# Both ends of a fused attention kernel: other orders and loads at the front, batch 0's transposes a step later, moves ahead of loads and two copies on VectorE at the end

## The chip, the core and the metric

The kernel runs on one core of one Trainium2 chip. The metric is the device time of one execution in microseconds. It was taken in three runs of the kernel, and one more execution was profiled. PE is TensorE, DVE is VectorE, ACT is ScalarE, POOL is GpSimd; SP issues most DMAs.

## What is computed

A residual attention layer over 64 batch items of 128 tokens with 512 features. There are 16 query heads of width 64 and one shared key and value head, with one extra "null" key and value in front of the 128 keys. The two layer norms use eps 1e-5.

```
xn   = layernorm(x) * g_in
q    = (xn @ Wq) as 16 heads of 64, times 1/8;  k, v = halves of (xn @ Wkv)
k, v = [null_k, k], [null_v, v]                       # 129 keys
sim  = q k^T + [null_bias, attn_bias]                 # 16 x 128 x 129
sim  = causal mask, and the batch item's key mask (the null key is always seen)
out  = softmax(sim) v, heads joined, @ Wo
y    = x + layernorm(out) * g_out
```

`null_k` and `null_v` are rows 0 and 1 of the input `cond`; all of it is 32-bit floating point.

## The kernel before

The function writes out, for each engine, one long list of instructions by hand. Each engine takes its own list in order and an instruction waits on semaphores for its inputs and for its buffers. So the order in which `step(n)` calls its helpers is the order on every engine, and an instruction that waits holds up all that is behind it on its engine.

**Steps.** The batch items come in 16 groups of four. The loop runs `step(n)` for n from -6 to 62. `step(n)` works on several items at once: it loads and normalises items some ten ahead, makes a part of the queries of group `(n + 6) // 4`, the keys and values of item n + 6, the scores of item `nb` (n + 2, later n + 3), the softmax of item `eb` (n + 1, later n + 2), the weighted sum of the values of item n, and the output projection of item n - 1 or of a pair of items. Steps -6 to 0 are the fill (`fill` in the code); here there are no values yet to be summed, and the queries of group 0 are plain products (`q_plain`, 3.4 us each, two in each of steps -6 to -3). From group 1 on, seven smaller products (`product`, with sums of tokens from `token_sum` and sums of weights from `weight_sums` and `weight_sum_3`) stand for eight. The output projections of items 1 to 58 are made for two items at a time in the same manner (`out_product`); item 0 and the items from 59 are made alone (`out_mm`, `out_stats`, `residual`). The constant `B3` is 58, and steps 57 to 61 have lines of their own.

**Normalising the input.** `norm_stats(m)` makes mean and variance on DVE and the reciprocal root on POOL (`pow`). `norm_apply(m)` scales on DVE for the first four items, on ACT from then on, with a factor `nmr` from DVE. `norm_T(m)` transposes on PE, and ACT copies the result out of PSUM. Items 8 and later go through a DVE transpose (`tokens_T`) and DMAs instead.

**Weights.** Each of the four parts of `wq` is scaled by `weights_q(kc)` (L842 to 850). The null key is worked into the key/value weights: POOL multiplies a part of `wq` with it (`weights_kv_prod`, L863), DVE scales `wkv`, sums the product and writes it in another order (`weights_kv`, `null_order`). `causal(u)` writes the causal mask into one half of the bias after its load.

**Softmax.** `bias_add` (POOL) writes bias plus key mask into the buffer `S[b]`, and `null_copy` (POOL) adds the null column; the tag "s" has two buffers. `scores` (PE) makes half of the scores, `scores_add` and `scores_max` (DVE) follow, `exps` takes one ACT instruction a row for eight rows in a half, and then come `rinv` (DVE) and `scale` (POOL). The scores live in one PSUM buffer of their own, so a second half waits for the first half's `scores_add`.

**Transposing the weights of attention.** Items 0 and 1 use PE: `attn_T_pe` (L606) transposes into PSUM and DVE copies to `aTb`. All later items use a DVE transpose (`blocks_T`, 1.77 us) and 14 small DMAs (`blocks_move`, L579), on SP's queue; for item 63 every second one goes to ACT's queue (`take`). `values` and `values_end` (PE) make the weighted sums, and ACT copies them out with the null value added (L680). In a step that goes on with scores, `values` waits for a tiny DVE copy, `done` (L668).

**Loads.** The loads of tokens, weights and bias are issued at the start; `load_second` (L175) follows when the first four items are under way, and `load_late` loads `wo` and `gob` after step -6. `transfers()` issues the stores of single items, residual loads and token loads of a step.

Of the kernel before, what the change touches and what calls it, by code (L numbers as in the profile page):

```python
# [17 lines left out]
def kernel(  # L18
# [156 lines left out]
    def load_second():  # L175
        nc.sync.dma_start(out=nbh, in_=null_bias.partition_broadcast(P))
        nc.sync.dma_start(out=nvb, in_=cond[1].partition_broadcast(P))
        load_mask(0)
        for m in (4, 5, 6):
            load_x(m)  # L180
        load_bias(1)
        for r in range(2):
# [206 lines left out]
    def weight_sum_3():  # L389
        nc.gpsimd.tensor_tensor(s3, a11, a21, ALU.subtract)  # L390
# [282 lines left out]
    def values_end(b, split):  # L673
# [5 lines left out]
        for u in range(2):  # L679
            nc.scalar.activation(  # L680
                oT[b][:, u * NF : (u + 1) * NF, :].rearrange(
                    "p f (s q) -> p s f q", q=Q
                ),
                po[u].rearrange("p h i f q -> p (h i) f q"),
                AF.Identity,
                bias=nv2,
            )
# [123 lines left out]
    def out_stats(b):  # L811
# [11 lines left out]
        if b == B - 1:  # L823

            nc.vector.scalar_tensor_tensor(y, y, rstd, res.pop(b), ALU.mult, ALU.add)
        else:
            yr[b] = y, rstd
# [8 lines left out]

    def store(b):
# [4 lines left out]
    def weights_q(kc):  # L842
        if kc < 2:
# [18 lines left out]
    def weights_kv_prod(kc):  # L862
        prods[kc] = sp.tile([P, H, DH], FP, tag="s", name=f"prod_{kc}")  # L863
# [15 lines left out]
    def step(n):  # L879
# [5 lines left out]
        mns = [m for m in (n + 10, n + 12) if ok(m) and (m >= 2 * GB) == (m == n + 12)]  # L885
# [27 lines left out]
        elif ok(nb) and n >= 0 and n != 1:  # L913
            bias_add(nb)
            null_copy(nb)
        if third:
            pair_pow(p4)
        for m in mns:
            norm_stats(m)
        if fast and f == 0 and fill:  # L920
            for k in range(1, 5):
                token_sum(qg, k)
            if n == -2:
                weight_sum_3()
# [3 lines left out]
        if ok(nb) and n < 0:  # L928
            null_copy(nb)
        if n == B3:  # L930
# [4 lines left out]
        if one:  # L935

            out_mm(n - 1, 0, NF if n > B3 + 1 else NC)
            if n == 1:
                attn_T_pe(1)
                bias_add(nb)  # L940
                null_copy(nb)
                out_stats(0)
# [11 lines left out]
        if soft:  # L954
# [17 lines left out]
        if soft:  # L972
# [3 lines left out]
        if soft and n != B3 + 1:  # L976
# [26 lines left out]
        if soft:  # L1003
# [8 lines left out]
        if n == B3:  # L1012
# [273 lines left out]
```

## Time and profile before

| what | before |
|---|---|
| three runs, us | 1126.49, 1126.77, 1124.78 |
| median, us | 1126.49 |
| the profiled execution, us | 1125.21 |
| its span, us | 1123.4 |
| PE busy | 1086.8 us, 97% of the span |
| DVE busy | 806.8 us, 72% |
| POOL busy | 745.0 us, 66% |
| ACT busy | 678.2 us, 60% |
| granted TensorE clock | 0.996 |

The profile shows one execution. Its page gives the busy time of each engine, and the busy share of each in 40 slices of 28 us. A row of the timeline is: start and duration in us, engine, line, operation, out and in with shapes, count, and in brackets the idle time of the engine just before it and what ended that. A row of the stretches gives the busy time of every engine between two points of the span, then the granted clock, the DMA share and the rate. Lines are those of the kernel before. Each 32-bit matrix product shows as two instructions. Neighbouring instructions of one kind are drawn together in one row, so a duration with a count above one spans all of them.

### The profile page before, as it was taken

The page shows a single profiled execution, that of the slowest core. Times are in us where ns is not written, and L with a number is a line of the kernel's source. Part 1 is how long each engine was busy: PE and PEld are TensorE (multiplying, and loading weights), DVE is VectorE, ACT ScalarE, POOL GpSimd, SP SyncE. Part 2 cuts the span into 40 slices and gives each one's busy share as a digit, 9 for nine tenths or more (in the row PEclk, how much of TensorE's full clock was granted, in tenths as well). Part 3 has the DMA queues.
Part 4 walks back from the last instruction along what each step waited for, and adds up shares of the span by engine and source line. Part 5 has one row for each costly group of instructions (what it writes and reads, how often), then busy time and mean ns, then how long its engine had stood idle before and what let it go on. Part 6 is the DMA issues. An engine that isn't in the chain of part 4 may idle for free.

```text
span 1123.4 us, 27505 instructions
## 1 busy us (share of the span) xinstructions
PE 1086.8 (97%) x9780; PEld 872.6 (78%) x9780; DVE 806.8 (72%) x1741; ACT 678.2 (60%) x2710; POOL 745.0 (66%) x588
## 2 busy tenths in 40 slices
PE   6888999999999999999999999999999999999987
PEld 4465788888888888888888888788888888888643
DVE  6564677786787777778777777877777886666762
ACT  2345656666675666676565667566567756657661
POOL 5454877667675676767577676657768575777832
PEclk9999999999999999999999999999999999999999
DMA  6313244353444435345343634534353453422333
GB/s 186 123 33 97 66 132 122 88 163 97 136 127 126 118 91 169 101 125 135 123 123 92 167 104 125 130 120 117 101 163 103 127 134 108 104 77 77 96 104 103
DMA packets 107864, 130.09 MB, mean 116 GB/s; under 512 B 29264, under 2 KB 72528, under 8 KB 105936
## 3 DMA queue, kind: packets, MB, share of 16 engines
q1 hardware_dynamic: 106480, 126.96, 40.1%
q8 instruction: 78, 1.28, 0.5%
q10 hardware_dynamic: 1248, 1.38, 0.4%
q14 instruction: 58, 0.48, 0.1%
HBM read 54.86 MB, written 31.46 MB: 77 GB/s over the span
## 4 chain that ended last, share of the span: by engine, by line
PE 82%; DVE 4%; DMA 4%; ACT 3%; POOL 2%; SPq 2%; issue 1%; ACTq 0%; POOLq 0%; DVEq 0%
PE pa L422 17%; PE pyX L750 16%; PE pyY L750 8%; PE pc L422 8%; PE ps L495 8%; PE po L636 7%; PE pk L308 5%; PE pw L422 4%; PE pyw L750 4%; PE py L697 3%; ACT s L522 2%; DMA x<-in_x_dram 2%; SPq L601 2%; DMA nbh<-cond_null_attn_bias_dram 1%; POOL xS L404 1%
## 5 line engine op out<-in xcount | busy, mean ns | idle before, releaser
L522 ACT ACTIVATE s<-s,nmax 128x65 f32<-128x65 f32 (+1 forms) x1024 | 372.1, 368 | 0.4
L466 POOL TENSOR_TENSOR s<-biasp,mneg 128x1536 f32<-128x1536 f32 x64 | 221.1, 3456 | 109.5 <-DVE sb L575 98.1
L543 POOL TENSOR_TENSOR s<-s,rinv 128x512 f32<-128x512 f32 (+1 forms) x128 | 189.3, 1480 | 119.3 <-DVE nmro L794 91.4
L680 ACT ACTIVATE oT<-po,nv 128x512 f32<-128x512 f32 x128 | 81.1, 684 | 199.4 <-PE po L636 199.4
L522 ACT ACTIVATION_READ_ACCUMULATOR s<-s,nmax 128x1 f32 x1024 | 194.6, 190 | 0.0
L750 PE MATMUL pyX<-wT,oT 128*128 128x256 f32 x696 | 164.7, 379 | 0.5 <-DVE kyu L762 0.5
L750 PEld LDWEIGHTS pyX<-wT,oT 128*128 128x128 f32 x696 | 131.8, 190 | 19.6 <-DVE kyu L762 0.9
L495 PEld LDWEIGHTS ps<-kT,qT 64*64 64x64 f32 x4096 | 94.5, 135 | 46.4 <-DVE s L508 24.2
L508 DVE TENSOR_TENSOR s<-ps,s 128x512 f32<-128x512 f32 (+1 forms) x128 | 121.5, 949 | 9.0 <-PE ps L495 8.7
L422 PE MATMUL pa<-xS,wq 128*128 128x256 f32 x480 | 123.7, 380 | 2.0 <-POOL wq L390 1.0
L513 DVE TENSOR_REDUCE nmax<-s 128x8 f32<-128x520 f32 (+1 forms) x128 | 120.1, 939 | 5.1 <-POOL s L475 3.7
L495 PE MATMUL ps<-kT,qT 64*64 64x64 f32 (+1 forms) x4096 | 118.9, 252 | 3.8 <-DVE s L508 3.1
L636 PE MATMUL po<-aTb,vs 64*64 64x256 f32 (+1 forms) x1240 | 118.5, 382 | 2.3 <-DVE done L668 2.2
L575 DVE STREAM_TRANSPOSE sb<-s 128x1536 f32<-128x1536 f32 x62 | 110.0, 1774 | 12.9 <-POOL s L543 3.6
L433 ACT COPY ku<-pa 128x256 f32<-128x256 f32 x120 | 44.8, 373 | 93.2 <-PE pa L422 93.2
L422 PEld LDWEIGHTS pa<-xS,wq 128*128 128x128 f32 x480 | 86.7, 190 | 12.3 <-ACT ku L433 1.6
L308 PE MATMUL pk<-wkv,xT 128*128 128x144 f32 x488 | 69.9, 286 | 0.0
L443 DVE TENSOR_TENSOR qT<-pw,kp 128x256 f32<-128x256 f32 x60 | 25.4, 424 | 61.4 <-ACT kp L433 61.3
L422 PE MATMUL pa<-xS,wS 128*128 128x256 f32 x240 | 67.8, 405 | 0.0
L636 PEld LDWEIGHTS po<-aTb,vs 64*64 64x64 f32 (+1 forms) x1240 | 57.0, 135 | 12.8 <-issue 3.9
L246 POOL TENSOR_TENSOR rstd<-rstd,nhalf 128x1 f32<-128x1 f32 x64 | 35.8, 560 | 42.9 <-DVE rstd L245 42.8
L422 PE MATMUL pc<-xS,wS 128*128 128x256 f32 x240 | 61.9, 380 | 1.9 <-POOL xS L404 1.9
(120 smaller groups left out, 2101.1 us busy)
## 6 DMA issues: line engine op xcount, KB each, us to landing
aTb<-sb SPq DMA_DIRECT2D x369, 64.0 KB
x<-in_x_dram SPq DMA_DIRECT2D x64, 256.0 KB
res<-in_x_dram SPq DMA_DIRECT2D x64, 256.0 KB
out_dram<-y SPq DMA_DIRECT2D x64, 256.0 KB
aTb<-sb SPq DMA_DIRECT2D x492, 32.0 KB
xd<-xb SPq DMA_DIRECT2D x14, 1024.0 KB
xT<-xd SPq DMA_DIRECT2D x56, 256.0 KB
wo<-in_L_cond_Wo_dram SPq DMA_DIRECT2D x1, 2048.0 KB
```

What stands on the lines that cost most here:

```text
L308: nc.tensor.matmul(pkv, xT[g][:, t, kc, :], wkv[:, kc, :], start=(kc == 0), stop=(kc == KC - 1),)
L422: nc.tensor.matmul(prod[tag], w[:, kc, f * P : (f + 1) * P], t[:, :, kc, :], start=(start and kc == 0), stop=(kc == HK - 1), skip_group_ch ...
L466: nc.gpsimd.tensor_tensor(S[b][:, :, 1 : ROW - 1], biasp, mneg[g][:, t].unsqueeze(1).broadcast_to([P, R8, NL + N]), ALU.add,)
L495: nc.tensor.matmul(pv[u * DH : (u + 1) * DH, r, f, :], qT[g][rows, f, t, hf, u], kT[b][rows, 0:nk], start=True, stop=True,)
L508: nc.vector.tensor_tensor(sv, pss.pop((b, hf)), sv, ALU.add)
L513: nc.vector.tensor_reduce(nmax[b][:, hf], S[b][:, :, WITH_NULL[hf]], AX.X, ALU.max, negate=True)
L522: nc.scalar.activation(row, row, AF.Exp, bias=nmax[b][:, hf, k : k + 1], accum_out=rsum[b][:, hf, k : k + 1],)
L543: nc.gpsimd.tensor_tensor(sv, sv, rinvs.pop((b, hf)).unsqueeze(2).broadcast_to([P, R8, sv.shape[2]]), ALU.mult,)
L575: nc.vector.transpose(sb.rearrange("p j e q -> p e j q"), S[b][:, :, 1 : ROW - 1].rearrange("p e (j k) -> p e j k", k=Q),)
L636: nc.tensor.matmul(pos[b][u][r * DH : (r + 1) * DH, half], vals[keys, b % GB, 0:DH], aT_of(b)[keys, slots, r * NF : (r + 1) * NF], start=s ...
L680: nc.scalar.activation(oT[b][:, u * NF : (u + 1) * NF, :].rearrange("p f (s q) -> p s f q", q=Q), po[u].rearrange("p h i f q -> p (h i) f q"),
L750: nc.tensor.matmul(prod[key], h[:, c, :], w[:, c, :], start=(start and c == 0), stop=(c == HC - 1), skip_group_check=not start,)
```

## The change

The front gets another order of loads, weights and norms. VectorE scales three parts of `wq` and ACT one; VectorE makes `weight_sum_3`; item 6 is normalised a step earlier, and its transpose keeps its place; the null value's negation, the null biases, the clearing of `aTb` and the loads of `wo` come later. The transposes of item 0 move from the end of step -1 into step 0, and bias and exponentials of items 1 to 3 get other places. At the end, the copies of items 61 and 62 are VectorE's, the moves of item 60 are split over two queues, moves come ahead of `transfers()`, several operations of steps 58 to 61 change places, and the last item's output is made in two halves of 256 columns.

```diff
 def load_second():
-    nbh; nvb; load_mask(0); x 4, 5, 6; load_bias(1); nv2
+    x 4, 5, 6; load_bias(1); load_mask(0); nbh; nvb; nv2
 def weight_sum_3():
-        nc.gpsimd.tensor_tensor(s3, a11, a21, ALU.subtract)
+        nc.vector.tensor_tensor(s3, a11, a21, ALU.subtract)
 def values_end(b, split):
         for u in range(2):
+            if b in (B - 3, B - 2):
+                nc.vector.tensor_scalar(o, v, nv2, None, ALU.add)
+            else:
+                nc.scalar.activation(o, v, AF.Identity, bias=nv2)
 def weights_q(kc):
-        if kc < 2:
+        if kc != 1:
             nc.vector.tensor_scalar(
 def weights_kv_prod(kc):
-        prods[kc] = sp.tile([P, H, DH], FP, tag="s", name=f"prod_{kc}")
+        pool, tag = ((sp, "s"), (sp, "s"), (hp, "sb"), (hp, "xb"))[kc]
+        bufs = None if kc < 2 else 1
+        prods[kc] = pool.tile([P, H, DH], FP, tag=tag, name=f"prod_{kc}", bufs=bufs)
+def last_output():
+        b = B - 1
+        halves = []
+        st = small.tile([P, 2, 6], FP, tag="st2", name="st2", bufs=1)
+        for e, (pool, tag) in enumerate(((ps_y, "Y"), (ps_w, "w"))):
+            cols = (lo_e, hi_e)[e]
+            py = pool.tile([P, HE], FP, tag=tag, name=f"py_{b}_{e}")
+            for c in range(NC):
+                nc.tensor.matmul(py, oT[b][:, c, :], wo[:, c, cols],
+                    start=(c == 0), stop=(c == NC - 1))
+            nc.vector.bn_stats(st[:, e], py)
+            halves.append((py, cols))
+        ...
+        for py, cols in halves:
+            nc.vector.scalar_tensor_tensor(
+                y[:, cols], py, mv[:, 0:1], gob[:, cols], ALU.subtract, ALU.mult)
+        r = res.pop(b)
+        for py, cols in halves:
+            nc.vector.scalar_tensor_tensor(
+                y[:, cols], y[:, cols], rstd, r[:, cols], ALU.mult, ALU.add)
+            nc.sync.dma_start(out=out[b][:, cols], in_=y[:, cols])
 def step(n):
-        mns = [m for m in (n + 10, n + 12) if ok(m) and (m >= 2 * GB) == (m == n + 12)]
+        mns = [... and m != 6]
-        elif ok(nb) and n >= 0 and n != 1:
+        elif ok(nb) and n > 1:
             bias_add(nb)
             null_copy(nb)
+        if fast and f == 0 and fill:
+            if n == -2:
+                weight_sum_3()
+            for k in range(1, 3):
+                token_sum(qg, k)
         for m in mns:
             norm_stats(m)
-        if fast and f == 0 and fill:
-            for k in range(1, 5):
-                token_sum(qg, k)
-            if n == -2:
-                weight_sum_3()
         ...
         if ok(nb) and n < 0:
             null_copy(nb)
+        if fast and f == 0 and fill:
+            for k in range(3, 5):
+                token_sum(qg, k)
         ...
             if n == 1:
                 attn_T_pe(1)
-                bias_add(nb)
-                null_copy(nb)
-                out_stats(0)
         ...
         if last:
             product(last_g, last_f, 4, ps_q, "a", start=False)
-        if soft:
+        if n == 1:
+            exps(eb, 0)
+            rinv(eb, 0)
+            scale(eb, 0)
+            exps(eb, 1, 0, 4)
+            bias_add(nb)
+            null_copy(nb)
+            out_stats(0)
+        elif soft:
             exps(eb, 0, 0, 4)
         ...
             q_out(last_g, last_f, hi_t, "c", "u2")
+        if n == 0:
+            attn_T_pe(0)
+            bias_add(nb)
+            null_copy(nb)
         ...
         if n == B3:
             scores(eb, 0)
             scores_add(eb, 0)
             scores_max(eb, 0)
             out_product(p12, 2, ps_w, "w")
+            out_part(p12, 0, "w", "yp1")
             pair_norm(p4)
+            scores(eb, 1)
+            scores_add(eb, 1)
             pair_residual(p4)
             store(p4)
-            out_part(p12, 0, "w", "yp1")
-            scores(eb, 1)
-            scores_add(eb, 1)
             exps_half(eb, 0)
-            scores_max(eb, 1)
         ...
             exps(eb, 1, 6)
-            rinv(eb, 1)
-            scale(eb, 1)
-        if third and n != B3:
+            if n <= B3 + 1:
+                rinv(eb, 1)
+                scale(eb, 1)
+        if third and n < B3:
             pair_norm(p4 + 1)
         ...
         if n == B3 + 1:
             blocks_T(n + 1)
-            blocks_move(n + 1)
+            blocks_move(n + 1, take=0)
         if soft and second:
             exps(eb, 1, 4)
+            if n == B3 + 1:
+                blocks_move(n + 1, take=1)
         ...
         if ok(n + 1) and fill:
-            exps(n + 1, 1)
+            exps(n + 1, 1, 0, R8 if n == 0 else 2)
         if sc and n != B3:
             scores(nb, 0)
             scores_add(nb, 0)
-            if ok(n + 1) and fill:
-                rinv(n + 1, 1)
-                scale(n + 1, 1)
         if ok(n):
             values(n, split)
+        if n == 0:
+            rinv(1, 1)
+            scale(1, 1)
+        if n == B3 + 2:
+            pair_norm(p4 + 1)
+            rinv(eb, 1)
+            scale(eb, 1)
         ...
-        if soft:
+        if soft and n != B3 + 3:
             blocks_T(eb)
         ...
             keep("a", "u2")
+        if n == -1:
+            exps(0, 1, 2)
         if ok(n) and not split:
             values_end(n, split)
+            if n == B3 + 3:
+                rinv(eb, 1)
+                scale(eb, 1)
+                blocks_T(eb)
         if n == B3:
             out_sums(p12)
             scores(nb, 0)
             scores_add(nb, 0)
+            scores_max(eb, 1)
             pair_norm(p4 + 1)
             pair_residual(p4 + 1)
         ...
-        late = first and fast
+        late = fast and (first or n < 0)
         if sc:
             scores(nb, 1)
             scores_add(nb, 1)
+            if n == -1:
+                rinv(0, 1)
+                scale(0, 1)
         ...
+        if n > B3 and eb in sbs:
+            blocks_move(eb)
         if n >= B3:
             transfers()
         ...
-        if n == -1:
-            attn_T_pe(0)
 # the start
+    keep_busy(14)
     norm_stats(0)
-    norm_stats(1)
     norm_apply(0)
     norm_T(0)
+    norm_stats(1)
     norm_stats(2)
+    keep_busy(4)
     norm_apply(1)
     norm_T(1)
     norm_stats(3)
+    keep_busy(2)
     norm_apply(2)
     norm_T(2)
-    keep_busy(8)
+    keep_busy(2)
     norm_apply(3)
     norm_T(3)
-    keep_busy(10)
+    keep_busy(3)
     load_second()
     weights_q(2)
     weights_q(0)
     weights_q(3)
     weights_q(1)
-    nc.gpsimd.memset(aTb, 0.0)
-    for kc in range(2):
-        weights_kv_prod(kc)
-    nc.vector.tensor_scalar(vnb[:, 0:DH], nvb, -1.0, None, ALU.mult)
-    null_order(vnb[:, DH:], nbh)
-    causal(1)
-    load_bias(0)
+    weights_kv_prod(0)
     for n in range(-6, B - 1):
         step(n)
         if n == -6:
+            for kc in range(1, KC):
+                weights_kv_prod(kc)
+            causal(1)
+            load_bias(0)
             for kc in range(2):
                 weights_kv(kc)
-            for kc in range(2, KC):
-                weights_kv_prod(kc)
-            load_late()
         if n == -5:
             for kc in range(2, KC):
                 weights_kv(kc)
             causal(0)
             mask_neg(0)
+            nc.vector.tensor_scalar(vnb[:, 0:DH], nvb, -1.0, None, ALU.mult)
+            null_order(vnb[:, DH:], nbh)
+            norm_stats(6)
+            norm_apply(6)
             weight_sums()
+        if n == -4:
+            nc.gpsimd.memset(aTb, 0.0)
+            load_late()
 # the end
-    out_mm(B - 1)
-    out_stats(B - 1)
-    store(B - 1)
+    last_output()
```

More of the change, by code (lines that the diff above doesn't have):

```diff
@@ L175, in load_second @@
     def load_second():
-        nc.sync.dma_start(out=nbh, in_=null_bias.partition_broadcast(P))
-        nc.sync.dma_start(out=nvb, in_=cond[1].partition_broadcast(P))
-        load_mask(0)
         for m in (4, 5, 6):
@@ L181, in load_second @@
         load_bias(1)
+        load_mask(0)
+        nc.sync.dma_start(out=nbh, in_=null_bias.partition_broadcast(P))
+        nc.sync.dma_start(out=nvb, in_=cond[1].partition_broadcast(P))
         for r in range(2):
@@ L679, in values_end @@
         for u in range(2):
[L680 to L687, printed above, removed]
+            o = oT[b][:, u * NF : (u + 1) * NF, :].rearrange("p f (s q) -> p s f q", q=Q)
+            v = po[u].rearrange("p h i f q -> p (h i) f q")
+            if b in (B - 3, B - 2):
+                nc.vector.tensor_scalar(o, v, nv2, None, ALU.add)
+            else:
+                nc.scalar.activation(o, v, AF.Identity, bias=nv2)
     def out_mm(b, lo=0, hi=NC):
@@ L822, in out_stats @@
         )
[L823 to L827, printed above, removed]
+        yr[b] = y, rstd
         ys[b] = y
@@ L835, in residual @@
         nc.gpsimd.tensor_tensor(y, y, res.pop(b), ALU.add)
+    def last_output():
[6 more added lines that the diff above has]
+            for c in range(NC):
+                nc.tensor.matmul(
+                    py,
+                    oT[b][:, c, :],
+                    wo[:, c, cols],
+                    start=(c == 0),
+                    stop=(c == NC - 1),
+                )
+            nc.vector.bn_stats(st[:, e], py)
+            halves.append((py, cols))
+        mv = small.tile([P, 2], FP, tag="mvo", name=f"mvo_{b}")
+        nc.vector.bn_aggr(mv, st)
+        rstd = small.tile([P, 1], FP, tag="rstdo", name=f"rstdo_{b}")
+        nc.vector.tensor_scalar(rstd, mv[:, 1:2], EPS, None, ALU.add)
+        nc.gpsimd.tensor_tensor(rstd, rstd, nhalf, ALU.pow)
+        y = hp.tile([P, DIM], FP, tag="y", name=f"y_{b}", bufs=3)
+        for py, cols in halves:
+            nc.vector.scalar_tensor_tensor(
+                y[:, cols], py, mv[:, 0:1], gob[:, cols], ALU.subtract, ALU.mult
+            )
+        r = res.pop(b)
+        for py, cols in halves:
+            nc.vector.scalar_tensor_tensor(
+                y[:, cols], y[:, cols], rstd, r[:, cols], ALU.mult, ALU.add
+            )
+            nc.sync.dma_start(out=out[b][:, cols], in_=y[:, cols])
     def store(b):
@@ L884, in step @@
         mkv, mk, mb = n + 6, n + 5, n + 11
-        mns = [m for m in (n + 10, n + 12) if ok(m) and (m >= 2 * GB) == (m == n + 12)]
+        mns = [
+            m
+            for m in (n + 10, n + 12)
+            if ok(m) and (m >= 2 * GB) == (m == n + 12) and m != 6
+        ]
         q, f = ok(qg, NG), part
@@ L971, in step @@
                 tokens_out(mb // GB)
-        if soft:
+        if soft and n != 1:
             exps(eb, 0, 4)
@@ L975, in step @@
             token_sum(qg, 1)
-        if soft and n != B3 + 1:
+        if soft and n not in (1, B3 + 1):
             rinv(eb, 0)
@@ L1002, in step @@
             q_plain(qg, 2 * f)
-        if soft:
+        if soft and n != 1:
             exps(eb, 1, 0, 2)
@@ L1029, in step @@
             out_part(p12, 0, "w", "yp1")
-        if soft:
+        if soft and n != 1:
             exps(eb, 1, 2, 4)
@@ L1090, in step @@
             store(p4 + 1)
-        if soft:
+        if soft and n != B3 + 3:
             blocks_T(eb)
```

## The prediction

> **What bounds the kernel now.** I read the page's busy rows, then PE by stretches, then the timeline of the badly filled stretches, then the chain at the end.
>
> ```profile
> PE 1086.8 (97%) x9780; PEld 872.6 (78%) x9780; DVE 806.8 (72%) x1741; ACT 678.2 (60%) x2710; POOL 745.0 (66%) x588
> ...
> PE   6888999999999999999999999999999999999987
> ...
> 17.97:47.52 29.55, 26.02 (x88) 13.35 (x87) 19.62 (x43) 8.73 (x14) 16.66 (x13) 1.00 0.47 128
> 47.52:66.98 19.46, 16.51 (x125) 10.75 (x124) 7.70 (x24) 5.54 (x12) 10.69 (x10) 1.00 0.18 53
> 66.98:81.00 14.02, 11.93 (x141) 9.03 (x140) 10.55 (x24) 8.21 (x38) 3.67 (x4) 1.00 0.07 20
> 81.00:93.97 12.97, 10.80 (x130) 8.55 (x127) 7.93 (x17) 8.73 (x38) 8.88 (x6) 1.00 0.54 155
> 93.97:117.00 23.03, 21.40 (x182) 14.23 (x180) 12.43 (x26) 10.15 (x42) 11.74 (x9) 0.93 0.14 35
> ```
>
> PE is full from slice 5 to 38: the middle can't be shortened by order. Columns of the stretches: length, then busy PE, PEld, DVE, ACT, POOL. PE's idle time, length minus busy: 3.5 + 3.0 + 2.1 + 2.2 + 1.6 = 12.4 us between the first query product (17.97) and the end of step 1 (117.0). Before 17.97 PE has only four token transposes to do. These 12.4 us and part of the 17.97 are all that the front can give. The timeline says what holds it (start, duration; in brackets the wait before):
>
> ```profile
> 11.69 1.38 POOL L1215 MEMSET aTb<- 128x1536 f32 x1
> 11.77 1.57 DVE L253 TENSOR_SCALAR x<-x,mv,rstd 128x512 f32<-128x512 f32 x1 [0.44 <-POOL rstd L246]
> 13.27 1.40 DVE L844 TENSOR_SCALAR wq<-wq,gin 128x1024 f32<-128x1024 f32 x2
> 16.42 2.19 ACT L848 ACTIVATE wq<-wq,gin 128x1024 f32<-128x1024 f32 x2
> 17.97 7.03 PE L373 MATMUL pq<-xT,wq 128*128 128x512 f32 x16
> ...
> 25.23 2.42 DVE L872 TENSOR_SCALAR wkv<-wkv,gin 128x128 f32<-128x128 f32 x1
> ...
> 42.73 0.66 PE L268 MATMUL pxT<-ident,x 128*128 128x128 f32 x4 [2.24 <-ACT x L259]
> ...
> 63.44 2.35 POOL L390 TENSOR_TENSOR wq<-wq 128x1024 f32<-128x1024 f32 x1
> 65.98 0.69 DVE L513 TENSOR_REDUCE nmax<-s 128x8 f32<-128x520 f32 x1 [3.72 <-POOL s L475]
> ...
> 90.30 0.66 PE L636 MATMUL po<-aTb,vs 64*64 64x256 f32 x8 [2.17 <-DVE done L668]
> ...
> 104.75 0.37 ACT L440 COPY qT<-pa 128x256 f32<-128x256 f32 x1 [8.98 <-PE pa L422]
> ...
> 119.20 3.45 POOL L466 TENSOR_TENSOR s<-biasp,mneg 128x1536 f32<-128x1536 f32 x1 [3.16 <-DVE mneg L452]
> ```
>
> A plain VectorE scaling takes 0.54 (the first three tokens), but 1.57 beside the memset; a 128x128 one takes 0.28 alone and 2.42 beside a POOL product that starts at 25.21. So some VectorE forms wait until POOL's instruction ends. And an in-order engine is stopped by its first waiting instruction: DVE by batch 0's null column (3.72), PE by `done` queued behind a reciprocal (2.17), ACT for 8.98 behind a query copy while PE does 6.9 us of `out_mm(0)`. At the end:
>
> ```profile
> 1076.62 1.98 PE L495 MATMUL ps<-kT,qT 64*64 64x128 f32 x32 [2.31 <-DVE s L508]
> ```
>
> and in the chain of waits (start, us, what)
>
> ```profile
> 1079.45 7.21 PE py L697 x16
> ...
> 1107.34 10.51 PE py L697 x24
> ```
>
> From 1079.4 to 1117.9 PE is in the chain nearly alone; before it DVE stops PE once more.
>
> **The change part by part, front.** Times are my schedule for the new order from these durations, against the same point before.
>
> Start: without the memset, token 3's scaling is 0.54: done at 12.3. DVE then scales parts 2, 0, 3 of wq (0.74 each): 13.05, 13.8, 14.5; ACT only part 1 (1.14). The ACT queue's two parts have landed by 9 us, SP's by about 11. Transposes 0.60, copy 0.59: first query product at 13.7, 4.2 earlier. The 14 more keep-busy instructions (50 for 36, 0.11 each) fill PE's idle time: 0. Moving three loads behind x and bias costs nothing: mask, nbh and nvb are first read near 32 us, and the wait of DVE for nvb (1.27, then 3.4 of slowed small copies) goes.
>
> Steps -6 and -5: two query products (6.87) and a transpose of 0.6 each. Now products 1 to 3 of the null key run back to back on POOL, 17.1 to 24.2 (2.35 each), then causal(1) 1.7; four of DVE's eight small operations meet them and wait up to 2.4 each. DVE reaches token 5's statistics at about 26.5 (28.96 before; 24.4 if it gets two operations between POOL's). Its transpose comes at 29.2, 1 us after PE could do it; step -4 starts at 29.85 for 33.45: 3.6 earlier.
>
> Step -4: norm 6 now stands ahead of `weight_sums` (3.7 us DVE), so the 2.24 wait goes; next late is token 8's statistics and then kv_out, at about 40.0. PE's three key/value products end at 42.2 for 47.6: 5.4. After it the memset (1.38) and two bias adds (6.9) stand ahead of token 7's power on POOL: its transpose waits 0.8: 4.4. SP: wo and gob now follow x9 and stand ahead of x10, x11 and the nv moves; 2 MB at the 400 GB/s of the first loads is 5 us, wo is first read in step 0 over 25 us later, nv 13 us later: 0 (0.6 us of issue at most).
>
> Step -2: `weight_sum_3` leaves POOL (2.35) and is 1.22 on DVE by rows L385 to 387. Those ran while POOL was idle; now POOL's token sums run beside it. Here a rule speaks against the change: by the Trainium skill, "SBUF — State Buffer", section Who interferes with whom, a DVE instruction with two SBUF inputs contends with a GpSimd instruction that reads SBUF, and the second waits. By the row DVE pays 1.2, by the rule up to 2.5 (one token sum of 1.27 more); no row here shows this pair. I take 1.3, keep 2.5 for the range: the sum falls from 11 to about 10. The null column now stands ahead of token sums 3 and 4, so the 3.72 goes, and product 7 has no 1.0 wait. End of step -2 at 59.4 for 66.98: 7.5.
>
> Steps -1 and 0: the transposes of batch 0 (2.1 us PE) move from -1 to 0 behind two products, so they no longer wait for the scale (0.9), but bias_add(2) (3.45) moves behind them too. Splitting exps 2+6 lets product 6's copy pass 2.3 us of ACT. Still ACT: 16 exps (5.8), copies and a norm make -1 end at 69.1, and the next product waits 1.2 for its last copy. Step 0: rinv(1,1) behind `values` ends the 2.17 wait, but values_end's copies stand behind eight exps, 1 us of PE. End at 84.2 for 93.97: 9.8.
>
> Step 1: exps(2, first half) and four more pass the query copy of 8.98 wait and run during `out_mm(0)`. DVE's rinv waits behind batch 1's transposed copies, so POOL starts with its scale only at about 94.3, then bias_add(3), power, scale, residual, weight sum: 10.8 us. PE ends at 103.9 for 117.0: 13.1. But DVE (maximum, kT, mask) ends 2 us later in relation to PE, so bias_add(4) comes at 108.1 for 119.2: 11.1. From here POOL is 99% busy for 30 us and leads the chain to the product at 134.8, so 11.1 is what remains. Later steps to 57 keep their order: 0.
>
> **End.** Step 58: out_part ahead of pair_norm frees the bank for which PE waited 0.9, but scores_max(60,1), 1.23, comes before pair_residual(56), for which PE waits next at about 1055.5 as before: 0 (-1 to +1). Step 59: half of batch 60's moves on the ACT queue: seven issues took 4.86 there for batch 63 (row of 1095.72); ACT was idle 3.50 before oT(59). So oT(59) and exps(62) come 1.3 late, of which I put 0.6 on PE; ends 0 and 4.9. SP is freed of 4.6 and the moves pass loads that blocked it 3.4: relief. Step 60: rinv and pair_norm(58) behind the score add: 0.2 for the two and 0.92 of waiting for exps go, -1.1. Two oT copies on DVE (about 0.7 each, idle there) let PE start without 0.32, and moves ahead remove an issue wait of 0.27. The last output: two halves of 8 products, the same 6.9 us; statistics of one half 0.42 for 0.70, then 0.2, 0.2 and four passes of 0.45 instead of two of 0.75: 2.6 us for 2.6; a last store of half the size, -0.1. Sum: -1.1 - 0.3 - 0.3 - 0.1 + 0.6 = -1.2.
>
> Together -12.3. The profiled execution took 1125.21 (span 1123.4 and 1.8 around it); 1112.9. It lies 1.3 under the median 1126.49, which would give 1114.2. I say 1113.5, 12.3 under 1125.8, the middle of the two.
>
> **Rivals.** (a) POOL holds the gain back: the wait for scale(2,0) at the head of POOL's queue in step 1 plus the lock of DVE; POOL starts step 2's chain only 4 us earlier. For it: 99% POOL to 150 us; against: POOL was idle 5.88 in step 1. 1125.8 - 4 - 1.2 = 1121. (b) DVE gets two operations between POOL's and ACT's waits shrink: nearly all of PE's 12.4 goes, with the 4.2 of the start 15, and 2 at the end: 1125.8 - 17 = 1109. (c) Slower: POOL in steps 0 and 1. bias_add(2) now waits for batch 0's transposes and bias_add(3) for scale(2,0), which waits for DVE behind batch 1's. Each us by which bias_add(4) slips is one at the end; it decides once bias_add(4) starts after 119.2 + 1.2 instead of 108, so 12.3 us of slip, from a chain whose own work is 10.8. At 5 us past that point: 1131. The rows speak against it, since DVE and ACT inputs are ready before. (d) The orders don't bite, everything waits as before for something not seen: 1126.
>
> **Numbers.** Forecast 0.50, (a) 0.20, (b) 0.20, (c) 0.06, (d) 0.04. Faster 0.90, same 0.04, slower 0.06; 0.2%, 2.3 us, is about what a measurement of this kernel can tell from no change. The forecast's own bounds (two-input wait 1.3, T5 and T7 1.8, ACT issues 4.3) give 1109 to 1119; with most of (a) and (b) 1107 to 1121.5.
>
> **What would show it.** Right: first query product near 13.7; token 3's scaling 0.54; no 3.72 and 2.17 wait; exps(2) inside `out_mm(0)`; bias_add(4) near 108; PE's end 1.2 closer to it than 998.7 us. Wrong: wkv or null copies of 2.4 each past 27 us; bias_add(4) later than 114; POOL the cause of PE waits after 110; oT(59) waiting on ACT's issues by more than 2 us.

## The result and the profile after

The changed kernel takes 1121.75 us (median of 15 runs, 1117.86 to 1125.59) against 1126.7 (15 runs of before beside it): ratio 0.9949, 95% interval 0.9939 to 0.9959. That is faster by about 5 us (0.5%) where 12.3 were forecast. Its profiled execution took 1120.76 (span 1119.0, before 1123.4), so the two traces differ by 4.4 us in span, and the reading below accounts for those 4.4.

Busy time by engine and the chain of waits of the changed kernel, from its page:

```profile
PE 1089.1 (97%) x9810; PEld 879.0 (79%) x9810; DVE 811.7 (73%) x1750; ACT 673.8 (60%) x2705; POOL 742.9 (66%) x587
...
PE 65%; DMA 8%; SPq 8%; DVE 7%; POOL 4%; issue 4%; ACT 3%; ACTq 0%; DVEq 0%; POOLq 0%
```

PE's busy time has grown by 2.3 us (1086.8 before), less than that of the dummy products alone (9.02 us for 5.50). PE is still nearly all of the span, but DMA and SP's queue together make 16% of the chain that ended last; before it was 6%, and PE 82%.

The timeline of the front in the changed kernel (start, duration, engine, line), against the lines shown in the prediction:

```profile
12.47 2.07 DVE L874 TENSOR_SCALAR wq<-wq,gin 128x1024 f32<-128x1024 f32 x3
14.01 7.13 PE L373 MATMUL pq<-xT,wq 128*128 128x512 f32 x16
17.43 2.23 DVE L905 TENSOR_SCALAR wkv<-wkv,gin 128x128 f32<-128x128 f32 x1
...
56.35 1.42 DVE L390 TENSOR_TENSOR wq<-wq 128x1024 f32<-128x1024 f32 x1
56.76 2.13 POOL L404 TENSOR_TENSOR xS<-xT,xS 128x512 f32<-128x512 f32 x1
...
111.04 3.45 POOL L466 TENSOR_TENSOR s<-biasp,mneg 128x1536 f32<-128x1536 f32 x1 [2.79 <-DVE mneg L452]
```

The first query product starts at 14.01 for 17.97, as forecast (13.7). The add of batch 4's bias comes at 111.04 for 119.20, 8.2 earlier; 11.1 were forecast. The missing 3 us go in one place. Rows of POOL, ACT and PE around 40 us, in step -4 (those of other engines left out):

```profile
38.89 0.55 POOL L246 TENSOR_TENSOR rstd<-rstd,nhalf 128x1 f32<-128x1 f32 x1 [4.99 <-DVE rstd L245]
39.77 0.81 ACT L259 ACTIVATE x<-x,nmr,rstd 128x512 f32<-128x512 f32 x1 [4.30 <-issue]
40.49 0.56 ACT L380 COPY qT<-pq 128x512 f32<-128x512 f32 x1
40.96 0.58 ACT L269 COPY xT<-pxT 128x512 f32<-128x512 f32 x1
41.59 2.29 PE L308 MATMUL pkv<-wkv,xT 128*128 128x144 f32 x8 [3.83 <-ACT xT L269]
...
46.77 7.46 PE L373 MATMUL pq<-xT,wq 128*128 128x512 f32 x16
```

ACT takes its list in order. In it, the normalisation of token block 8 (L259) stands ahead of the query copy (L380) and of the transposed copy of block 6 (L269). Block 8's statistics come late, because DVE has 3.7 us of weight sums ahead of them and POOL's power follows at 38.89. So ACT stands idle for 4.30 with two copies ready behind the waiting instruction, and PE waits 3.83 for the second copy. It does not wait for its data: by the code, the second key/value product writes into the PSUM buffer that holds block 6's transposes (tag "w", two buffers), and the copy empties it. In the kernel before, block 8's normalisation stood ahead of the same copies:

```profile
41.86 1.62 ACT L259 ACTIVATE x<-x,nmr,rstd 128x512 f32<-128x512 f32 x2 [4.19 <-DVE nmr L258]
...
43.38 0.57 ACT L380 COPY qT<-pq 128x512 f32<-128x512 f32 x1
...
43.85 0.59 ACT L269 COPY xT<-pxT 128x512 f32<-128x512 f32 x1
...
47.52 7.03 PE L373 MATMUL pq<-xT,wq 128*128 128x512 f32 x16
```

There block 6's own normalisation came first and PE waited for that (2.24). The change moved block 6 ahead and left block 8 where it was. When PE goes on in the changed kernel, it is slow: 2.29 for eight instructions that take 1.15 elsewhere. The stretch from 40 to 50 us (length, busy PE, PEld, DVE, ACT, POOL, granted clock, DMA share, GB/s):

```profile
40.00:50.00 10.00, 8.00 (x25) 5.84 (x26) 3.59 (x14) 1.96 (x5) 8.43 (x5) 0.66 0.74 238
```

The granted clock is 0.66 there; in the trace it is one half from 40.80 for 6.83 us. The key and value products end at 46.77, where 42.2 was forecast and before had 47.52.

For the rest I cut each trace at two points that all kernels share, the start of the scores of item 4 and of item 60. Front is up to item 4; the middle, in which both kernels have the same order on every engine, lies between; the tail is from item 60 to the end of the span. The four points, before and then changed:

```profile
125.77 0.69 PE L495 MATMUL ps<-kT,qT 64*64 64x64 f32 x32
...
1045.74 0.69 PE L495 MATMUL ps<-kT,qT 64*64 64x64 f32 x32
```

```profile
117.60 0.69 PE L495 MATMUL ps<-kT,qT 64*64 64x64 f32 x32
...
1041.72 0.69 PE L495 MATMUL ps<-kT,qT 64*64 64x64 f32 x32
```

| | item 4 starts | middle | tail | span |
|---|---|---|---|---|
| before | 125.77 | 919.97 | 77.69 | 1123.4 |
| changed | 117.60 | 924.12 | 77.26 | 1119.0 |
| difference | -8.17 | +4.15 | -0.43 | -4.4 |

So the front brought 8.2 instead of 11.1, half of that was lost again in a middle that I had entered with 0, and the tail brought 0.4 instead of 1.2. Even the 0.4 is uncertain: the tail of before has 3.41 us at half clock in it (from 1076.31), that of the changed kernel has none until PE's last products are done.

### The profile page after: what moved, and what is told of

Same layout as the page of the kernel before. It is cut to its first block, busy times and chain, and to the rows that moved or that the text cites. A ratio compares the mean times of both kernels' runs of the same rounds, so it can differ in the third digit from the quotient of the medians.

```text
span 1119.0 us, 27573 instructions
## 1 busy us (share of the span) xinstructions
PE 1089.1 (97%) x9810; PEld 879.0 (79%) x9810; DVE 811.7 (73%) x1750; ACT 673.8 (60%) x2705; POOL 742.9 (66%) x587
## 4 chain that ended last, share of the span: by engine, by line
PE 65%; DMA 8%; SPq 8%; DVE 7%; POOL 4%; issue 4%; ACT 3%; ACTq 0%; DVEq 0%; POOLq 0%
PE pa L422 14%; PE pyX L749 12%; PE ps L495 6%; DMA x<-in_x_dram 6%; PE po L636 6%; PE pyY L749 6%; PE pc L422 6%; SPq L601 6%; PE pk L308 4%; PE pw L422 3%; PE pyw L749 3%; ACT s L522 2%; SPq L295 1%; DMA aTb<-sb 1%; PE py L696 1%
## 5 line engine op out<-in xcount | busy, mean ns | idle before, releaser
L686 ACT ACTIVATE oT<-po,nv 128x512 f32<-128x512 f32 x124 | 78.4, 683 | 197.6 <-PE po L636 191.4
L308 PEld LDWEIGHTS pk<-wkv,xT 128*128 128x128 f32 x488 | 63.5, 191 | 0.1
L803 ACT ACTIVATE yn<-y,nmro,rstdo 128x512 f32<-128x512 f32 x58 | 45.3, 781 | 29.1 <-DVE nmro L793 29.1
```

Of the source, the lines that this page charges most:

```text
L308: nc.tensor.matmul(pkv, xT[g][:, t, kc, :], wkv[:, kc, :], start=(kc == 0), stop=(kc == KC - 1),)
L686: nc.scalar.activation(o, v, AF.Identity, bias=nv2)
```

## The experiments

All times are medians, with the ratio to the kernel before in the same batch where there is one. Before itself had 1126.66, 1128.26, 1129.32 and 1128.31 in the four batches, so ratios compare better than times.

**The front alone and the tail alone.** The first is the changed kernel with every edit from step 58 on undone (its end is below), the second the kernel before with those edits alone.

```
-    last_output()
+    out_mm(B - 1)
+    out_stats(B - 1)
+    store(B - 1)
```

> The changed kernel with the last steps put back in the order of before; only the front is new. Theory A (the front's gain is 8.2 us at the scores of item 4, some 4 of it are lost in the middle, and the tail is worth 0.4): 4.0 us under the time before, about 1122.5. Rival B (the tail gives the 1.2 us of the prediction, the front 3.5): 3.3 under. Rival C (the tail costs time, because moves of item 59 and copies come late): 6 under. The scores of item 4 start at 117.6 as in the changed kernel in all three.

> The kernel before with only the last steps (from step 58) of the changed one. Theory A: 0.4 us under the time before, so not to be told from it (within 0.2%). Rival B: 1.2 to 2 us under. Rival C: 1 to 2 us over. PE's waits in the last 80 us should be those of the changed kernel (aTb of item 58, DVE oT of item 61 behind rinv(63)), if they belong to the tail's own order and not to the earlier start.

Front alone: 1121.28, ratio 0.9956 (0.9939 to 0.9972); item 4 at 115.74, middle 923.73, tail 77.60. Tail alone: 1127.54, ratio 1.0007 (0.9994 to 1.0019). The tail is worth nothing that can be told. B falls, since the tail alone gains nothing. C, a cost of 1 to 2 us, is not excluded here: the interval reaches 2 us, and the tail alone has 79.36 in its trace against 77.69 before, though with two stretches of 3.41 at half clock for one. PE's wait for the copy of oT(61) is 2.4 there, so it belongs to the tail's order and not to the earlier start. The tails are taken up again below. Item 4 came 1.9 earlier than expected; the half clock in step -4 lasted 3.41 us in that profile and not 6.83, and 3.41 us less at half clock are 1.7 us of work. The loss in the middle is there with the front alone.

**Block 8's normalisation later.**

```
         for m in mns:
-            norm_apply(m)
+            if n != -4:
+                norm_apply(m)
...
             norm_T(n + 10)
+        if n == -4:
+            norm_apply(8)
         if ok(mkv) and mkv >= GB - 1:
```

> The changed kernel, but in step -4 ACT's normalisation of token block 8 stands behind the query copy and the transposed copy of block 6 instead of ahead of them. Theory A1 (the in-order queue of ACT, waiting for block 8's statistics, holds back the copies that PE's key and value products wait for, and the wait of 3.8 us then brings the half clock): the wait of 3.8 and the half clock of 6.8 us near 41 go, the key/value products end at 42 to 43 instead of 46.8, the scores of item 4 start at 114 to 116 instead of 117.6, and the time is 2 to 4 us under the changed kernel. Rival D (the middle takes back what the front gains beyond some 4 us): key/value products end at 42 to 43 as well, but the time stays within 1 us of the changed kernel. Rival E (block 8 is only then the next thing to be late): PE waits as long a step later, and the scores of item 4 stay at 117.6.

1115.56, ratio 0.9908 (0.9892 to 0.9924): 11 us under before and 6 under the changed kernel, where 2 to 4 were expected (the two traces differ by 5.1). Its timeline, and the same stretch:

```profile
40.84 1.22 PE L308 MATMUL pkv<-wkv,xT 128*128 128x144 f32 x8
...
42.01 7.03 PE L373 MATMUL pq<-xT,wq 128*128 128x512 f32 x16
...
106.87 3.46 POOL L466 TENSOR_TENSOR s<-biasp,mneg 128x1536 f32<-128x1536 f32 x1 [2.78 <-DVE mneg L452]
...
40.00:50.00 10.00, 8.94 (x30) 4.63 (x31) 4.55 (x18) 3.13 (x6) 8.92 (x5) 1.00 0.80 255
```

The key and value products end at 42.01, the clock is full, and item 4 starts at 113.44, 12.3 us earlier than in the old kernel. The earlier start reaches the end: D and E fall, and A1 stands for the queue. Moving one call settles what stopped the front. Whether the half clock was the wait's doing is taken up below, since this kernel has neither.

**Earlier loads of x.** In the middle of the changed kernel some loads of x land late, so I gave them a fourth buffer and one step more.

```
-    XB = 3
+    XB = 4
...
-        for m in (n + 13, n + 14):
-            if m < B and (m > 2 * GB + 2) == (m == n + 14):
+        for m in (10, 11, 12) if n == -3 else (n + 13 + 2 * (n > -3),):
+            if m < B:
```

> The changed kernel with a fourth buffer for the blocks of x, so that from step -3 on each block is loaded one step (about 16.5 us) earlier; the buffer's room comes from scaling the null value in place. Theory F (the 4.2 us that are lost in the middle are late loads of x: SP issues them only some 9 us before the statistics): PE from the scores of item 4 to those of item 60 takes 920 us or less instead of 924.1, DVE's waits for x go, and the time is 3 to 5 us under the changed kernel. Rival G (the losses come from the moves of the transposed weights and of other data, the late x only shows where it is): 923 to 925 us, and the time within 1 us of the changed kernel.

1121.30, ratio 0.9956 (0.9939 to 0.9973); middle 922.84. Theory F falls. Late x was a sign of something else.

**The number of dummy products.** The page of the changed kernel shows the fetch of instructions as DMA traffic:

```profile
q8 instruction: 78, 1.28, 0.5%
```

That is 78 packets of 16 KB. The page counts 9810 matmuls and as many weight loads on PE; 19,620 divided by 78 is 252. By the Trainium skill, "Perfetto Trace Analysis", The 4-stage abstract model, an instruction has 64 bytes, so a packet holds 256: the count fits queue 8 being PE's code. In the trace PE starts 256 instructions between two packets on average, though not evenly. So instructions added ahead should shift the place of the fetch in all later steps. The change has 25 dummy products at the start for 18, which is 28 more instructions on PE. I took 7 out of the first group, where PE is idle anyway, and put 7 into the kernel before.

```
-    keep_busy(14)
+    keep_busy(7)
```

The kernel before, and the rival of places (unused first tiles, which bring every buffer to its old address):

```
+    keep_busy(7)
     norm_stats(0)
     norm_stats(1)
...
+    for tag, cols, bufs in (
+        ("vs", GB * (DH + H), 3), ("kT", N, 6), ("xb", KC * TOK, 1),
+        ("nv", GB * (DH + H), 2), ("y", DIM, 3), ("sb", 6 * R8 * Q, 1),
+    ):
+        hp.tile([P, cols], FP, tag=tag, name=f"pre_{tag}", bufs=bufs)
```

> The changed kernel with block 8's normalisation later (as in the last batch, 1115.56) and with 7 of its 25 dummy products taken out at the very start, where PE is idle anyway; before has 18 of them. What is open is why PE takes 922.8 to 924.1 us from the scores of item 4 to those of item 60 in every kernel with the new front, and 919.3 to 920.0 in the two with the old one, in the same order of work. Theory H (PE's instructions are fetched in packets of 16 KB, 1 us each on one DMA engine, once in 256 instructions; the new dummies and extra products shift where in a step the fetch falls, and it meets the moves of the transposed weights that PE waits for): with the old number of dummies, 919 to 920.5 us, and the time 2 to 3.5 us under 1115.56. Rival I (the buffers' places in SBUF) and rival J (the head start itself is lost against some other engine's pace): 922.5 to 924, and the time within 0.7 of 1115.56.

> The kernel before with 7 more dummy products at the start, where PE is idle: nothing else. Theory H: from item 4 to item 60 PE takes 922 to 924 us instead of 920, and the time is 2 to 4 us over before. Rivals I and J: 919 to 920.5 us, and the time that of before.

> The kernel with block 8's normalisation later, with every buffer at the SBUF address that it has before (the changed kernel's first use of two buffers for products of the null key moved them). Rival I: 919 to 920.5 us from item 4 to item 60, and 1112 to 1113.5. Theory H and rival J: 922.5 to 924, and 1115 to 1116.5.

> The changed kernel with 7 of its 25 dummy products taken out at the very start: nothing else. Theory H: 919.5 to 920.8 us from the scores of item 4 to those of item 60 (924.1 with 25), and the time 2.5 to 3.5 us under the changed kernel, about 1118.5. Rival J: 922.5 to 924, and the time within 0.7 us of it. PE's wait of 3.8 us in step -4 stays, and by theory K the half clock near 41 with it.

| kernel | dummies | middle | time, ratio to before |
|---|---|---|---|
| before | 18 | 919.97 | |
| before, new tail | 18 | 919.26 | 1127.54, 1.0007 |
| before + 7 dummies | 25 | 922.06 | 1130.01, 1.0015 (0.9997 to 1.0032) |
| changed | 25 | 924.12 | 1121.75, 0.9949 |
| changed - 7 dummies | 18 | 920.36 | 1119.14, 0.9925 (0.9906 to 0.9943) |
| front alone | 25 | 923.73 | 1121.28, 0.9956 |
| earlier x | 25 | 922.84 | 1121.30, 0.9956 |
| block 8 later | 25 | 922.85 | 1115.56, 0.9908 |
| block 8 later, old places in SBUF | 25 | 923.64 | 1116.7 (one run) |
| block 8 later, - 7 dummies | 18 | 920.51 | 1115.44, 0.9881 (0.9844 to 0.9918) |

With 18 dummies the middle takes 919.3 to 920.5 (919.45 to 920.59 in the three kernels of the tail below), with 25 it takes 922.1 to 924.1, whichever front, tail or buffers stand beside it. The three kernels of the next part, with 36 and 43 dummies, have 922.62, 921.77 and 924.03. None of these traces has half clock in the middle but the last (3.41 us from 384.49), so the clock is not the reason. Rivals I and J fall. Seven products of no use, in time that nobody needs, cost 2 to 4 us some 200 to 900 us later. The times show it less well: the kernel before is slower by 1.7 us with 7 more, but the interval includes no change. Nor do those of the pair with block 8 later tell it (four runs each, and the one with 18 had the lower clock, 0.991 to 0.999 against 0.997 to 1.0). The ratios of the changed kernel's own pair differ by 2.7 us, its traces by 3.8.

Where a part of it happens can be seen at PE's values of one item. The DMA traffic and PE's timeline, first of block 8 later with 25 dummies (379.0 to 381.7 us), then with 18 (377.0 to 379.2 us):

```profile
q8 instruction: 1, 0.02, 3.2%
...
381.76 0.43 PE L636 MATMUL po<-aTb,nv 64*64 64x256 f32 x2 [1.44 <-DMA aTb<-sb]
```

```profile
q14 instruction: 2, 0.02, 2.8%
...
379.21 0.43 PE L636 MATMUL po<-aTb,nv 64*64 64x256 f32 x2
```

In the first, one packet of queue 8 stands between the last move of the transposed weights and the values that read it. It takes 3.2% of 16 engines' 2.7 us, 1.38 us of one engine, and PE waits 1.44 for the moves. In the second no packet of queue 8 falls there (the next one starts at 380.77), and PE doesn't wait. All five traces with the new front and 25 dummies have a wait of 1.24 to 1.69 at this item, with a packet of queue 8 some 2 to 3 us ahead of the values. The changed kernel is one of them (1.60 at 386.17, packet at 383.45); with 18 dummies it does not wait there. In the kernel before with 25 dummies no packet stood there (the last came 12 us ahead), these values lost nothing, and its 2.1 us are spread over many items.

That the packet holds back a move on its own DMA engine would fit, but no trace row names the engine, and other traces speak against it. The kernel before (0.64) and those with 36 and 43 dummies (0.80; 1.19 and 1.86) wait at the same item, and the last packet of queue 8 started over 5 us ahead of the values in each. The one with the longest wait, its DMA traffic from 380.5 to 383.5 us:

```profile
q1 hardware_dynamic: 277, 0.31, 34.3%
q14 instruction: 2, 0.02, 1.9%
...
383.46 0.43 PE L636 MATMUL po<-aTb,nv 64*64 64x256 f32 x2 [1.86 <-DMA aTb<-sb]
```

So it is shown that the number of dummies moves the length of the middle, and that with more of them one item waits longer for its moves. How the number does it is open; theory H's packets alone do not explain it.

**Filling the wait.** Three tries with 18 dummies (3.9 us) in PE's list in step -4 of the changed kernel.

```
             for m in range(GB - 1):
+                if m == 1:            # m == 2 in the first try
+                    keep_busy(18)
                 kv_out(m, kv_mm(m))
```

> The changed kernel, block 8's normalisation where the change has it, with 18 dummy products (some 3.9 us) in PE's list ahead of the key/value product that waits 3.8 us in step -4. Theory K (the half clock of 3.4 to 6.8 us after that wait is the answer to PE's idleness): no half clock near 41, the key/value products end 1.5 to 2.2 us earlier than in the changed kernel (46.77), at about 45, though the copy comes no sooner. Rival L (the half clock falls there by its own course, or follows from what ran before the wait): half clock as in the changed kernel, end at 46.8 or later. The time tells less, since 72 more instructions on PE shift the fetches of theory H as well.

> The changed kernel with 18 dummy products (some 3.9 us) in PE's list ahead of the second key/value product of step -4, where PE really waits (the last batch's stood one product too late, behind the wait). Theory K (the idleness brings the half clock): none near 41, and key/value products end at about 44.5. Rival L (it comes by another course): half clock of 3.4 us or more between 40 and 46, as it came in the kernel with block 8 later and 18 dummies after a wait of only 1.6 us.

> The same with 18 dummy products ahead of the second key/value product of step -4, so that PE waits there with work in hand (25 dummies in all, but 18 of them later). Theory K: no half clock between 40 and 46, key/value products end at about 44.5. Rival L: half clock as in the kernels with the wait, end at 45.3 to 46.8.

(The third has 36 dummies in all, not 25.) The first try was misplaced: PE still waited 3.25 ahead of the dummies and the clock was half from 42.52 for 3.41, so it says nothing for K or L (1123.84, ratio 0.9962). The second (1117.88, one run) and third have the dummies where PE waits. The third, with 7 fewer at the start (1117.33, ratio 0.9910, 0.9885 to 0.9935):

```profile
37.20 4.18 PE L1259 MATMUL busy<-ident 128*128 128x128 f32 x36
41.30 1.25 PE L308 MATMUL pkv<-wkv,xT 128*128 128x144 f32 x8
...
40.00:50.00 10.00, 9.49 (x45) 6.04 (x44) 4.19 (x15) 3.67 (x8) 8.32 (x5) 1.00 0.73 232
```

The product starts hardly sooner than in the changed kernel (41.59; 41.39 with 18 dummies and the wait not filled), yet runs in 1.25 for 2.29, and the stage ends at 44.34 for 46.77 (44.57 in the second try). Over all traces, the five kernels with a wait of 3.25 to 3.93 had half clock from 40.8 to 42.9 on, for 3.41 or 6.83 us; of nine with waits of 0.67 to 2.68 at that place two had it (41.61 and 44.68); the two with the wait filled had none. So K holds, for about 2.3 us of the stage's end: PE's idleness there brought the half clock. The rule of the Trainium skill ("TensorE: Matmul & The Clock Gate", What's actually happening) is that a window of some 3.4 us without work halves the clock. The durations of 3.41 and 6.83 fit such windows, but the waits of 1.63 and 2.68 are shorter than one, and so is that of 3.25.

The traces settle it. In each, all starts of half clock lie on one grid of 3.41 us, to within 0.01 us. I cut all 16 traces into these windows, from 12 us to PE's last product, and took PE's busy time in each. All 24 starts follow a window in which PE was busy for 1.78 us or less. After windows of 1.40 or less half clock came 15 times in 15, after 1.48 to 1.78 9 times in 19, and after fuller ones never, in some 5,000. So here a window need not be empty: PE idle for about half of it can be enough, and whether a wait of 1.6 us costs clock depends on how it falls on the grid. Half clock stayed for a second window where PE was busy for 1.97 to 2.79 of the first, and ended after one window where it was busy for 3.00 or more.

**The tail.** Block 8 later and 18 dummies in all three; first the old tail, then the new one with two orders mended, then the new one with the copies of oT(61) and oT(62) back on ACT.

```
-        if soft and n not in (1, B3 + 1):
+        if soft and n not in (1, B3 + 1, B3 + 3):      # rinv, scale of the first half
...
             if n == B3 + 3:
+                rinv(eb, 0)
+                scale(eb, 0)
                 rinv(eb, 1)
...
             exps(eb, 0, 4)
+            if n == B3 + 3:
+                residual(n - 2)
...
-        if one and n > 1:
+        if one and n > 1 and n != B3 + 2:
             residual(n - 1)
```

The third:

```
-            if b in (B - 3, B - 2):
+            if b is None:
                 nc.vector.tensor_scalar(o, v, nv2, None, ALU.add)
             else:
                 nc.scalar.activation(o, v, AF.Identity, bias=nv2)
```

> The kernel with block 8's normalisation later and 18 dummies, with the last steps in the order of before. The tail is taken from the start of the scores of item 60 to the end of the span: 77.7 us in the kernel before, 77.3 in the changed one, 77.6 with block 8 later and the new tail. Theory M (the new tail is worth nothing, since two of its orders cost what two others bring): 77.3 to 78 here as well, time within 1 us of the same kernel with the new tail. Rival N (the tail gives 1.2 us, but the other runs' clock hides it): 78.5 to 79.

> The kernel with block 8's normalisation later, 18 dummies and the new tail, with two orders mended: VectorE's copies of oT(61) stand ahead of the reciprocal of batch 63's first half instead of behind it, and ACT does 8 of batch 63's exponentials ahead of the scaling of output 59. Theory M: PE's wait for oT of 1.49 us and part of ACT's 8.2 us of idleness ahead of output 59 go, and the tail is 1.5 to 3 us shorter: 74.6 to 76.1. Rival O (the chain of batch 63, exponentials, reciprocal, scale, transposes, moves, takes over at its values): 0 to 0.8 shorter, with a wait of PE for the moves of batch 63 of 1.5 us or more instead of 0.7.

> The kernel with block 8's normalisation later, 18 dummies and the new tail, with the copies of oT(61) and oT(62) back on ACT. The prediction gave their move to VectorE 0.3 us of gain. Theory M (they stand behind a reciprocal on DVE that waits for ACT's exponentials, 1.49 us of PE): tail 0.5 to 1.5 us shorter than 77.6. Rival P (on ACT they stand behind the exponentials themselves): 0.3 us longer or more.

Old tail: 1114.69, ratio 0.9877 (0.9855 to 0.9899), the same as with the new one (0.9881). Its tail in the trace is 79.27 with one stretch of half clock in it, the new one's 78.59 with one as well. The 79.27 lies outside the ranges of both M and N, so the comparison must be made without half clock. The old tail has 77.60 then (front alone, the one such trace), the new one 77.10 to 78.23 (seven traces). So M holds: the new tail is worth nothing that can be told, and C's cost of 1 to 2 us does not show either. One of the longest waits of PE in the changed kernel (total, times, longest) is of the tail and new:

```profile
PE py L696 <- DVE oT L684: 1.9, 1, 1.9
```

In the kernel with block 8 later it is seen on DVE and PE:

```profile
1081.99 0.20 DVE L539 RECIPROCAL rinv<-rsum 128x8 f32<-128x8 f32 x1 [3.49 <-ACT s L522]
1082.11 1.36 DVE L684 TENSOR_SCALAR oT<-po,nv 128x512 f32<-128x512 f32 x2
1082.87 3.70 PE L696 MATMUL py<-wo,oT 128*128 128x512 f32 x8 [1.49 <-DVE oT L684]
```

DVE stands 3.49 before a reciprocal that needs ACT's exponentials of batch 63, with the copy that PE waits for behind it. With the two orders mended:

```profile
1076.53 7.13 PE L696 MATMUL py<-wo,oT 128*128 128x512 f32 x16
...
1077.13 1.40 DVE L684 TENSOR_SCALAR oT<-po,nv 128x512 f32<-128x512 f32 x2
```

the copies come in time, no wait stands ahead of this product, and all 16 instructions run in one piece. The tail is 75.26, 2.3 shorter than the 77.59 of block 8 later; time 1110.39, ratio 0.9841 (0.9820 to 0.9863), 4.3 under the old tail in the same batch, whose trace has half clock in it. O falls. What each of the two orders gives was not taken apart. This is the fastest kernel of the study. With the copies on ACT instead the time is 1119.24, ratio 0.9921 (0.9897 to 0.9945), and PE waits 3.46 for oT at 1084.85, where it waited 1.49 to 1.88 with VectorE's copies. So P holds by the wait: within the new order the copies are better on VectorE. How much time that is isn't shown; the ratio's interval meets that of the same kernel with VectorE's copies (0.9844 to 0.9918). That kernel also ran at a lower clock (0.989, half for 17 us of its tail), so its 84.37 us of tail are not the price of the copies alone.

## Why the prediction was wrong, and where it was right

**Right, the schedule of the front but for one stage.** The start (14.01 for 13.7), token 5's transpose (28.82 for 29.2), the 3.72 and 2.17 waits gone, batch 2's exponentials inside `out_mm(0)`. Where the wait of step -4 is taken away, my later steps come out one by one: key/value products end at 42.01 (42.2 forecast), step -2 at 59.34 (59.4), the product after step -1 at 69.91 after a wait of 0.52 (69.1 and a wait of 1.2), step 0 at 83.41 (84.2), batch 4's bias at 106.87 (108.1).

**Wrong, step -4.** "Next late is token 8's statistics and then kv_out, at about 40.0": I saw that block 8 is late, but priced it by the engine that computes it. I did not ask what stands behind its normalisation on ACT: two copies, one of which empties the buffer that PE's second key/value product needs. Before, PE waited there for block 6 anyway; with block 6 moved ahead, block 8 became the wait, of 3.83 us, and a half clock came with it, which I had not entered at all. The term was 5.4 us gained; it measured 0.75 (47.52 to 46.77). Part of the loss came back, because later steps then waited less: 8.2 at item 4 for 11.1.

**Wrong, the dummies: "50 for 36 ... fill PE's idle time: 0".** Their time is indeed free at the start. Their instructions are not: 2 to 4 us of the middle, shown in the traces by taking them out of the changed kernel and by putting them into the kernel before. This is also why "later steps to 57 keep their order: 0" failed: the order is the same, and the middle took 4.15 more. By what path the instructions do it stays open. I had also read PE's row of nines as a middle that order can't change; it ran from 919.26 to 924.12 in kernels with that same order.

**Too large, the tail: -1.2 for -0.4 or nothing.** I had the oT copies wait for nothing on an idle DVE; idle it is, but in front of a reciprocal that waits for ACT. That took 1.5 to 1.9 us in the new front's traces, more than the whole tail was to bring. The rest of the tail's terms was not taken apart.

**The rivals.** Rival (a) gave 1121, near the result, by another mechanism: POOL holding the gain back. With block 8 later, POOL's list in steps 0 and 1 is the same, and batch 4's bias came 4.2 earlier at once; POOL did not hold it, and the rival's number was near by luck. For the two-input rule the trace sides with the Trainium skill ("SBUF — State Buffer", Who interferes with whom): DVE's weight sum, which began while a token sum of POOL ran, took 1.42 for 1.22, and POOL's next token sum, which began while the weight sum ran, 2.13 for 1.27. I took 1.3 on DVE, which is about right; POOL paid 0.86, which I had not entered.

In sum: of the 12.3 us forecast, 2.9 were lost in the front, 4.15 in the middle and 0.8 in the tail; what is left is the 4.4 between the two traces. With the three mended, the kernel is 1.6% under before, some 18 us.

## What to carry to other kernels

When a change takes away one wait, find the instruction that waits next, list what stands behind it on the same engine, and who needs that, for its data or for its buffer; an in-order engine passes on its wait to all of it. A stop of PE can be paid a second time in clock, here when PE was idle for about half of a window of 3.41 us. The number of instructions is not free where their time is: in this kernel of 20,000 PE instructions, 7 dummy products at the start moved the middle by 2 to 4 us, so compare orders at an equal count, or try a few counts. Cut the traces at points that both kernels share before looking for causes; here it showed at once that half of the loss lay where nothing had been edited.

## What the runs showed of the hardware

- 78 packets of 16 KB come on queue 8 during the execution, one for 256 PE instructions on average, which fits PE's code. With 7 dummy products more or fewer, the middle of the kernel differs by 2 to 4 us. One packet took 1.38 us of a DMA engine and PE waited 1.44 for data moved beside it, but PE waited 1.86 at the same item where no packet stood; what the fetch does to other transfers is not shown.
- Half clock came in pieces of 3.41 or 6.83 us: in five of five traces after PE had waited 3.25 to 3.93, in two of nine after 0.67 to 2.68, in none of two where dummies filled the wait. Over all traces it began only on a grid of 3.41 us, after windows in which PE was busy for at most 1.78 us: always at 1.40 or less, about every second time from 1.48 to 1.78.
- A VectorE sum with two SBUF inputs and POOL's token sums slow each other: 1.42 us for 1.22 on VectorE, 2.13 for 1.27 on POOL.
